# Sums over five chunks in one PSUM bank at loaded addresses, 16 single table lines a chunk and 72 VectorE column copies

## The chip, the core and the metric

The kernel runs on one core of a Trainium2 chip. The metric is the device time of one execution in microseconds (us). Five engines work beside each other, each through its own queue in order: TensorE (PE, with its weight loads shown as PEld), VectorE (DVE), ScalarE (ACT), GpSimd (POOL) and SyncE (SP). In this kernel POOL and SP only issue transfers once the main loop runs.

## What is computed

A graph layer with 12,500 nodes of 48 features and 400,000 edges, sorted by their target node `dst`. The source nodes `src` are random.

```python
h = jnp.maximum(_layernorm(x), 0.0)
tmp = jnp.concatenate([h[dst], h[src], edge_attr], axis=1)   # 48 + 48 + 32
hid = jax.nn.relu(tmp @ W1 + b1)                             # 128 wide
msg = hid @ W2 + b2
x = x + jax.ops.segment_sum(msg, dst, num_segments=12500)
```

Since W1 acts on three parts apart, the kernel first makes two node tables: `tab_a` (W1's part for `dst`, with b1) and `tab_b` (its part for `src`). The product with W2 is taken after the sum over the edges of a node: the sum of `hid` and the number of edges (for b2) are all that it needs.

## The kernel before

**Stages.** `node_tables` makes the two tables in DRAM, and a transposed copy `bt` of `tab_b` in SBUF. Then `windows` runs over 391 chunks of 1,024 edges, a chunk being 8 tiles (`T`) of 128 edges. As the edges are sorted, the targets of a chunk lie within a window of 80 nodes (`W`).

**One chunk.** SP brings 80 rows of `tab_a` (`rhs`), the edge features (`lhs`, rows 80 to 111) and the targets (`row`). DVE compares the targets with the window's nodes into the other rows of `lhs` (line 458) and into `hot`, a 0/1 matrix of edges by window nodes (line 464; its other operand `wnum`, the numbers of the window's nodes, lies in a PSUM bank of its own). PE multiplies `lhs` and `rhs` into `pre` (`before`, line 476). DVE adds the rows of `tab_b` and applies the maximum with 0 into `hid` (lines 506, 513 and 515). PE multiplies `hid` with `hot` (`fold`, line 524) for the sums of `hid` by node, and `ones` with `hot` (line 529) for the numbers of edges.

**Three ways to bring a row of `tab_b`.** Most tiles of a chunk are gathered by POOL, one indirect transfer a tile (line 442; 2,631 in all). 458 tiles are brought as columns of `bt` that are copied one by one within SBUF (line 384): 151 columns a chunk, 71 by DVE and 80 by ACT, in nine parts (`PARTS`). Each part first reads its columns' addresses into registers (line 349, TENSOR_LOAD). PE turns such a tile and adds it to `pre` (`turned`, line 485). 36 tiles are brought by SP, line by line: 12 transfers of 512 bytes a chunk (`singles`, line 416), which DVE adds to `pre` (line 504).

**The sum over chunks.** `fold` leaves the sums of one chunk in a fresh PSUM tile `p_g`. DVE adds it into `seg`, a buffer in SBUF of 1,024 nodes, at the window's place (`add`, line 543). After 12 chunks (`GQ`) DVE moves the overlap to the other buffer and clears the rest (`segment_next`, lines 559 and 561). PE multiplies the buffer with W2, half by half (`segment_sum`, lines 569 and 570), DVE adds that to `xseg`, the segment's part of x (line 571), and SP stores it (line 575) after having loaded it (line 552).

**Order.** The order is written out by hand: in the pass for chunk c the engines make `prepare(c)` (transfers, `lhs`, `hot`), `before(c-1)`, `fold(c-2)`, `turned(c-1)`, the segment's work, `gathered(c-1)`, `hidden(c-1)` and `add(c-2)`, with the column copies between them. SP's transfers share eight completion semaphores in turn, so each waits until the one eight before it has landed. `rhs` has three buffers, as has `lhs`; `gb`, where POOL's rows land, has eight; a column tile `gt` five.

Of the kernel before, what the change touches and what calls it, by code (L numbers as in the profile page):

```python
# [16 lines left out]
P = 128  # L17
# [12 lines left out]
GQ = 12  # L30
OFF = -(NCH - 3) % GQ
L = 1024
# [3 lines left out]
BLK = 512  # L36
STORE = 2
# [18 lines left out]
    (True, 0, 19, 1),  # L56
    (True, 19, 20, 20),
    (True, 39, 16, 40),
    (True, 55, 16, 56),
    (False, 71, 16, 72),  # L60
    (False, 87, 16, 88),
    (False, 103, 16, 104),
    (False, 119, 16, 120),
    (False, 135, 16, 136),
# [6 lines left out]
SEG0 = 130848  # L71
SEG_SIZE = 8 * L
# [3 lines left out]
PLACE0 = 156  # L76
SINGLE = 12
SINGLE_AT = 160
WIDTH = 172
# [199 lines left out]
def windows(nc, tc, gp, bt, ident, idx, x_t, tab_a, tab_b, dst, edge_t, w1, w2s, b2s, out_t):  # L279
# [3 lines left out]
    with ExitStack() as es:  # L283
        seg = es.enter_context(tc.tile_pool(name="segs", bufs=1))

        segs = [seg.tile([P, 2, L], F32, name=f"seg{k}") for k in range(2)]
# [6 lines left out]
        ps_g = es.enter_context(tc.tile_pool(name="ps_g", bufs=2, space=PSUM))  # L293
        ps_f = es.enter_context(tc.tile_pool(name="ps_f", bufs=1, space=PSUM))
        xp = es.enter_context(tc.tile_pool(name="xp", bufs=2))
        ps_w = es.enter_context(tc.tile_pool(name="ps_w", bufs=1, space=PSUM))


        wnum = ps_w.tile([P, W], F32, name="wnum")
# [16 lines left out]
        place = PARTS[0][3] - 1  # L316
        for a, b in ((place, SEG2), (NEXT, SEG)):
# [4 lines left out]
        at_place = slice(place, place + 1)  # L322
        nc.vector.scalar_tensor_tensor(
            last[:, :, at_place], last[:, :, at_place], 4.0, last[:, :, PLACE0 : PLACE0 + 1],
            op0=ALU.mult, op1=ALU.add,
        )
        for seg in segs:
            nc.vector.memset(seg, 0.0)
# [9 lines left out]
        def group(c):  # L338

            return divmod(c + OFF, GQ)  # L340

        def begin(g):
            return max(0, g * GQ - OFF)

        def numbers(c, at, n, engine):

            got = []
            for k in range(0, n, MOST):
                got += nc.values_load_multi_w_load_instructions(  # L349
                    last[c % P : c % P + 1, c // P, at + k : at + min(k + MOST, n)],  # L350
                    engines=[engine], min_val=0, max_val=1 << 23,
                    skip_runtime_bounds_check_because="numbers of nodes, and what is made of them",
                )[1]
            return got

        def node(n):
            return n.with_bounds(min_val=0, max_val=N - 1)
# [3 lines left out]
        def load(c, part):  # L361

            dve, first, n, at = PARTS[part]
            n = max(0, min(n, len(BYCOLS) * P - ((c - COLS) * PART + first))) if c >= COLS else 0
            engine = mybir.EngineType.DVE if dve else mybir.EngineType.Activation
            if part == 0 and 2 <= c < NCH + 2:
                base, *nodes = numbers(c, at - 1, n + 1, engine)
                st[c - 2]["base"] = base
            else:
                nodes = numbers(c, at, n, engine) if n else []  # L370
            regs[c, part] = nodes
# [19 lines left out]
        def mark(ins, us):  # L391
            marks.append((ins, us))
# [77 lines left out]
        def before(c):  # L470

            s = st[c]
            n = s["n"]
            pre = ps_p.tile([P, T, HID], F32, name="pre")
            for t in range(n):
                nc.tensor.matmul(  # L476
                    pre[:, t, :], s["lhs"][:K, t * P : (t + 1) * P], s["rhs"][:K, :],
                    start=True, stop=t not in turned_at(c),
                )
            s["pre"] = pre  # L480
# [37 lines left out]

        def fold(c):
            s = st[c]  # L520
            n = s["n"]
            p_g = ps_g.tile([HID, 2, W], F32, name="p_g")
            for t in range(n):
                nc.tensor.matmul(  # L524
                    p_g[:, 0, :], s["h"][:, t, :], s["hot"][:, t, :], start=t == 0, stop=t == n - 1
                )
            high = s["hot"].bitcast(BF16)
            for t in range(n):
                nc.tensor.matmul(  # L529
                    p_g[:, 1, :], ones, high[:, t, 1::2], start=t == 0, stop=t == n - 1  # L530
                )
            s["p_g"] = p_g

        def add(c):

            s = st.pop(c)
            k = group(c)[0] % 2
            of = SEG0 + k * SEG_SIZE
            at = s["base"].with_bounds(
                min_val=of, max_val=of + 4 * FAR, guaranteed_mod_val=0, out_of_modulus=4  # L540
            ) - of
            to = segs[k].bitcast(U8)[:, :, bass.ds(at, 4 * W)].bitcast(F32)
            mark(nc.vector.tensor_add(to, to, s["p_g"]), 0.25)  # L543

        xs = {}
# [8 lines left out]
        def segment_next(g):  # L554

            old, new = segs[g % 2], segs[(g + 1) % 2]
            if g > 0:
                for k in range(2):
                    nc.vector.memset(new[:, k, W:], 0.0)  # L559
            of, = numbers(begin(g), NEXT, 1, mybir.EngineType.DVE)  # L560
            nc.vector.tensor_copy(
                new[:, :, :W], old[:, :, bass.ds(of.with_bounds(min_val=0, max_val=FAR), W)]
            )

        def segment_sum(g, k, n):

            seg, s = segs[g % 2], slice(k * BLK, k * BLK + n)
            p_f = ps_f.tile([D, BLK], F32, name="p_f")
            nc.tensor.matmul(p_f[:, :n], w2s, seg[:, 0, s], start=True, stop=False)  # L569
            nc.tensor.matmul(p_f[:, :n], b2s[:1, :], seg[:1, 1, s], start=False, stop=True)  # L570
            nc.vector.tensor_add(xs[g][:, s], xs[g][:, s], p_f[:, :n])  # L571

        def segment_store(g, n):
            first, = numbers(begin(g), SEG, 1, mybir.EngineType.SP)
            nc.sync.dma_start(out_t[:, bass.ds(node(first), n)], xs.pop(g)[:, :n])

        with tc.manual_schedule():
            for c in range(NCH + 2):
# [8 lines left out]
                if 0 <= c - 1 < NCH:  # L587
                    before(c - 1)
                if 0 <= c - 2 < NCH:
                    fold(c - 2)  # L590
                if 0 <= c - 1 < NCH:
                    turned(c - 1)

                g, k = group(c - 2)
                if k == GQ - 3 or c == NCH - 1:
                    segment_load(g)
                if g > 0 and k < L // BLK:
                    segment_sum(g - 1, k, BLK)
# [9 lines left out]
                if 0 <= c - 2 < NCH:  # L608
                    add(c - 2)
                    if k == GQ - 1:  # L610
                        segment_next(g)
                columns(c, 3)
                for part in range(DVE_PARTS, len(PARTS)):
                    load(c, part)
                    columns(c, part)
                if c == NCH + 1:
                    segment_sum(g, 0, END_L)
                    segment_store(g, END_L)
# [342 lines left out]
```

## Time and profile before

| | us |
|---|---|
| median of 3 runs | 3562.99 (3554.6 to 3570.09) |
| the profiled execution | 3548.53 |
| its span, first to last instruction | 3546.7 |
| busy: PE / DVE / ACT / POOL | 2628.1 / 3258.7 / 3123.8 / 2667.2 |
| DVE column copies (27,584) / ACT column copies (31,040) | 1818.8 / 3077.3 |
| mean granted TensorE clock | 0.784 of full |

Durations of successive instructions of an engine overlap a little, so what one costs is read from its start to the next one's start. SP has no line of busy time; the timeline shows the transfers that it issues, each with the time that the issue took. A bracket at the end of a timeline row gives the idle time ahead of it and what ended it.

### The profile page before, as it was taken

How to read it: one execution, taken by the hardware profiler on the slowest of the kernel's cores; microseconds unless marked ns; L12 is line 12 of the kernel's file. 1: busy time of each engine (PE TensorE's matmuls, PEld its weight loads, DVE VectorE, ACT ScalarE, POOL GpSimd, SP SyncE). 2: the span in 40 equal slices, each digit the busy share in tenths (PEclk: the TensorE clock that was granted, in tenths of full speed). 3: DMA queues.
4: the chain of work that ended last, by engine and by line, in shares of the span. 5: the costliest groups of instructions: out<-in, count | busy, mean ns of one | idle time of the engine just before them, and what ended most of it. 6: DMA issues, size and time to landing. Idle time of an engine off the chain costs nothing.

```text
span 3546.7 us, 119948 instructions
## 1 busy us (share of the span) xinstructions
PE 2628.1 (74%) x17111; PEld 2359.2 (67%) x17111; DVE 3258.7 (92%) x30218; ACT 3123.8 (88%) x31115; POOL 2667.2 (75%) x2658
## 2 busy tenths in 40 slices
PE   8677677777777776777777777777777777777777
PEld 6566666667666766666667666666666666666666
DVE  6799999999999999999999999999999999999997
ACT  5898989899898898988999899998988899898884
POOL 5777777777777777777777777777777777777773
PEclk9677887786777778877787778777787788777777
DMA  5533333333333333333333333333333333333332
GB/s 201 164 97 99 96 93 94 93 93 102 95 93 92 95 90 103 95 96 93 92 95 97 97 96 96 95 92 93 99 95 93 95 91 93 103 96 94 91 95 58
DMA packets 197246, 349.05 MB, mean 98 GB/s; under 512 B 67763, under 2 KB 104517, under 8 KB 195157
## 3 DMA queue, kind: packets, MB, share of 16 engines
q0 software_dynamic: 84224, 172.62, 19.2%
q1 hardware_dynamic: 111952, 168.56, 15.8%
q14 instruction: 670, 5.48, 0.5%
q8 instruction: 140, 2.29, 0.3%
q10 hardware_dynamic: 260, 0.10, 0.0%
HBM read 321.55 MB, written 22.07 MB: 97 GB/s over the span
## 4 chain that ended last, share of the span: by engine, by line
DVE 68%; PE 8%; ACT 6%; issue 5%; DVEq 4%; DMA 3%; SPq 0%; ACTq 0%; POOL 0%; POOLq 0%
DVE gt L384 38%; DVE hid L506 8%; ACT gt L384 6%; DVE hot L464 6%; DVE lhs L458 5%; DVE hid L513 5%; DVEq L349 4%; PE p_g L524 4%; DMA gb<-tab_b,srci 3%; DVE seg L543 2%; DVE hid L515 2%; PE p_f L569 1%; PE p_f L570 1%; PE pre L476 1%; PE pre L485 1%
## 5 line engine op out<-in xcount | busy, mean ns | idle before, releaser
L384 ACT COPY gt<-bt 128x1 f32 x31040 | 3077.3, 187 | 334.0 <-PE pre L485 226.2
L442 POOL DMA_INDIRECT gb<-tab_b,srci x2631 | 2645.7, 1006 | 822.5 <-issue 371.7
L384 DVE COPY gt<-bt 128x1 f32 x27584 | 1818.8, 144 | 161.1 <-issue 104.3
L524 PE MATMUL p_g<-hot,hid 128*128 128x80 f32 x6250 | 1074.6, 344 | 873.8 <-DVE hid L513 873.4
L524 PEld LDWEIGHTS p_g<-hot,hid 128*128 128x128 f32 x6250 | 1004.6, 252 | 950.1 <-DVE hid L513 940.9
L476 PEld LDWEIGHTS pre<-rhs,lhs 112*128 112x128 f32 x6250 | 964.9, 243 | 86.1 <-issue 85.2
L476 PE MATMUL pre<-rhs,lhs 112*128 112x128 f32 x6250 | 994.1, 327 | 16.5 <-DMA lhs<-in_edge_t 16.3
L506 DVE TENSOR_TENSOR hid<-pre,gb 128x896 f32<-128x896 f32 (+2 forms) x391 | 408.7, 1045 | 0.6
L464 DVE TENSOR_TENSOR hot<-wnum,rel 128x640 f32<-128x640 f32 x391 | 318.2, 814 | 0.0
L458 DVE TENSOR_SCALAR lhs<-row,bw 80x1024 f32<-80x1024 int16 x391 | 290.2, 742 | 9.2 <-DMA row<-in_dst 9.2
L485 PE MATMUL pre<-ident,gt 128*128 128x128 f32 x916 | 270.2, 403 | 9.8 <-DVE gt L384 9.6
L513 DVE TENSOR_SCALAR hid<-hid 128x896 f32<-128x896 f32 (+2 forms) x391 | 243.0, 622 | 0.1
L529 PE MATMUL p_g<-hot,ones 128*128 128x80 bf16 x3125 | 239.4, 237 | 0.0
L529 PEld LDWEIGHTS <-ones 128*128 128x128 bf16 x3125 | 239.1, 132 | 0.0
L485 PEld LDWEIGHTS pre<-ident,gt 128*128 128x128 f32 x916 | 192.4, 269 | 11.2 <-issue 11.2
L543 DVE TENSOR_TENSOR seg<-seg,p_g 128x160 f32 x391 | 124.5, 318 | 15.1 <-issue 11.4
L515 DVE TENSOR_SCALAR hid<-pre 128x128 f32<-128x128 f32 (+1 forms) x389 | 118.7, 305 | 0.0
L569 PE MATMUL p_f<-seg,w2s 128*48 128x512 f32 (+1 forms) x134 | 106.5, 890 | 0.4 <-DVE seg L543 0.4
L571 DVE TENSOR_TENSOR xseg<-xseg,p_f 48x512 f32<-48x512 f32 (+1 forms) x67 | 45.0, 672 | 50.8 <-PE p_f L570 50.7
L570 PE MATMUL p_f<-seg,b2s 1*48 1x512 f32 (+1 forms) x134 | 86.6, 731 | 0.0
L570 PEld LDWEIGHTS p_f<-seg,b2s 1*48 1x48 f32 x134 | 12.4, 135 | 87.6 <-issue 87.6
L559 DVE MEMSET seg<- 128x944 f32 x64 | 54.1, 845 | 9.3
(67 smaller groups left out, 294.7 us busy)
## 6 DMA issues: line engine op xcount, KB each, us to landing
gr<-tab_b SPq DMA_DIRECT2D x4608, 0.5 KB
row<-in_dst SPq DMA_DIRECT2D x390, 160.0 KB
lhs<-in_edge_t SPq DMA_DIRECT2D x390, 128.0 KB
gb<-tab_b,srci POOLq DMA_INDIRECT x2631
rhs<-tab_a SPq DMA_DIRECT2D x391, 40.0 KB
xseg<-in_x_t SPq DMA_DIRECT2D x33, 192.0 KB
out_x<-xseg SPq DMA_DIRECT2D x33, 192.0 KB
tab_b<-tab SPq DMA_DIRECT2D x3, 1280.0 KB
```

What stands on the lines that cost most here:

```text
L384: done = copy(gts[of][:, e : e + 1], bt8[:, bass.ds(at, 4)].bitcast(F32))
L442: fetch = nc.gpsimd.indirect_dma_start(out=gb[:, t, :], out_offset=None, in_=tab_b[:, :], in_offset=bass.IndirectOffsetOnAxis(ap=srci[:, c ...
L458: mark(nc.vector.tensor_scalar(lhs[:W, : n * P], row[:, : n * P], bw[:, c : c + 1], None, op0=ALU.is_equal,), 0.8)
L464: mark(nc.vector.tensor_tensor(hot[:, :n, :], wnum.unsqueeze(1).to_broadcast([P, n, W]), rel[:, c * T : c * T + n].unsqueeze(2).to_broadca ...
L476: nc.tensor.matmul(pre[:, t, :], s["lhs"][:K, t * P : (t + 1) * P], s["rhs"][:K, :], start=True, stop=t not in turned_at(c),)
L485: nc.tensor.matmul(st[c]["pre"][:, t, :], gts.pop(j), ident, start=False, stop=True)
L506: mark(nc.vector.tensor_add(to, of, rows), 1.0)
L513: mark(nc.vector.tensor_scalar(of, of, 0.0, None, op0=ALU.max), 0.55)
L515: nc.vector.tensor_scalar(apart(c, s["h"], True), apart(c, s["pre"], True), 0.0, None, op0=ALU.max)
L524: nc.tensor.matmul(p_g[:, 0, :], s["h"][:, t, :], s["hot"][:, t, :], start=t == 0, stop=t == n - 1)
L529: nc.tensor.matmul(p_g[:, 1, :], ones, high[:, t, 1::2], start=t == 0, stop=t == n - 1)
L543: mark(nc.vector.tensor_add(to, to, s["p_g"]), 0.25)
```

## The change

- **Fewer chunks to a segment, and the sum on PE.** A segment is now 5 chunks and 432 nodes. Its sums lie in one PSUM bank (`sums`), the edge numbers in another (`degs`), two of each in turn. `segment_begin` clears both by a product of zeros. `fold` reads two addresses into PE's registers and adds each product into the bank there. `add` and `segment_next` are gone.
- **The segment's end.** ACT copies the banks to SBUF (`segment_copy`, first chunk of the next segment), PE multiplies with W2 into the same bank (`segment_product`, second chunk), DVE copies the 80 overlapping nodes from the last `xseg` and adds the product (`segment_sum`, third chunk), SP stores it in the fifth. Before, store and load came once in 12 chunks; now each comes once in 5.
- **Where a row comes from.** `SINGLE` goes from 12 to 16 lines a chunk, DVE's columns from 71 to 72. 48 tiles come by lines, 461 by columns and 2,616 by POOL. DVE's parts are 16, 20, 20 and 16 columns, where they were 19, 20, 16 and 16.
- **One bank shared.** `wnum`, which `hot` is made from, now lies in the bank of the first of the two `degs` (tile `deg0`).

```diff
-GQ = 12
+GQ = 5
-L = 1024
+L = 432
-STORE = 2
+STORE = 4
...
-SINGLE = 12
+SINGLE = 16
...
+        sums = [ps_s.tile([P, L], F32, name=f"sum{k}") for k in range(2)]
+        beside = ps_w.tile([P, L + W], F32, name="deg0")
+        degs = [beside[:, :L], ps_w.tile([P, L], F32, name="deg1")]
+        wnum = beside[:, L:]
...
+        def segment_begin(g):
+            for of in (sums[g % 2], degs[g % 2]):
+                nc.tensor.matmul(
+                    of, zeros[:, :P], zeros, start=True, stop=False, skip_group_check=True
+                )
...
         def fold(c):
...
-            p_g = ps_g.tile([HID, 2, W], F32, name="p_g")
+            for at, of, first in zip(
+                numbers(c, PLACE, 2, mybir.EngineType.PE), (sums[k], degs[k]),
...
+                to.append(of.bitcast(U8)[:, bass.ds(at, 4 * W)].bitcast(F32))
             for t in range(n):
                 nc.tensor.matmul(
-                    p_g[:, 0, :], s["h"][:, t, :], s["hot"][:, t, :], start=t == 0, stop=t == n - 1
+                    to[0], s["h"][:, t, :], s["hot"][:, t, :], start=False, stop=False,
...
-            mark(nc.vector.tensor_add(to, to, s["p_g"]), 0.25)
...
+        def segment_copy(g):
+            sm[g] = segp.tile([P, 2, L], F32, name="seg")
+            nc.scalar.copy(sm[g][:, 0, :], sums[g % 2])
+            nc.scalar.copy(sm[g][:1, 1, :], degs[g % 2][:1, :])
...
+        def segment_product(g, n):
+            seg, p_f = sm.pop(g), out_of(g, n)
+            nc.tensor.matmul(p_f, w2s, seg[:, 0, :n], start=True, stop=False, skip_group_check=True)
...
+        def segment_sum(g, n):
             if g > 0:
-                for k in range(2):
-                    nc.vector.memset(new[:, k, W:], 0.0)
...
+                nc.vector.tensor_copy(
+                    xs[g][:, :W],
+                    xs[g - 1][:, bass.ds(of.with_bounds(min_val=0, max_val=FAR), W)],
+                )
+            nc.vector.tensor_add(xs[g][:, :n], xs[g][:, :n], out_of(g, n))
```

**On SP**, a chunk's transfers and a store of a segment in the middle of the loop, before (line 416 brings single lines, line 575 stores):

```order
L427 DMA rhs_717<-tab_a 80x512
L432 DMA lhs<-in_edge_t 32x1024
L434 DMA row<-in_dst 80x1024
L349 TENSOR_LOAD last
L416 DMA gr<-tab_b 1x512 x12
L349 TENSOR_LOAD last
L575 REGISTER_ALU
L575 DMA out_x<-xseg 48x1024
```

and with the change (lines 411 and 582):

```order
L422 DMA rhs_712<-tab_a 80x512
L427 DMA lhs<-in_edge_t 32x1024
L429 DMA row<-in_dst 80x1024
L349 TENSOR_LOAD last
L411 DMA gr<-tab_b 1x512 x16
L349 TENSOR_LOAD last
L582 REGISTER_ALU
L582 DMA out_x<-xseg 48x432
```

The row of lines grew from 12 to 16; a store (and a load, written alike) stands there every fifth chunk, with a read of a number ahead of it.

**On PE**, one chunk's `before` and the start of its `fold`, with the semaphores waited for, before:

```order
L476 MATMUL pre_25892<-rhs0_713,lhs_25166 128x128 x7
L524 MATMUL p_g_25901<-hot_24681,hid_25366 128x80 [waits DVE_49]
L524 MATMUL p_g_25901<-hot_24681,hid_25366 128x80 x6
L524 MATMUL p_g_25901<-hot_24681,hid_25366 128x80 [waits DVE_49]
L529 LDWEIGHTS ones_88
L529 MATMUL p_g_25901<-hot_24681,ones_88 128x80
```

and with the change, in a segment that uses `deg0`:

```order
L471 MATMUL pre_24982<-rhs0_712,lhs_24229 128x128 x7
L349 TENSOR_LOAD last_87
L535 MATMUL sum0_690<-hot_23718,hid_24444 128x80 [waits DVE_49]
L535 MATMUL sum0_690<-hot_23718,hid_24444 128x80 x6
L535 MATMUL sum0_690<-hot_23718,hid_24444 128x80 [waits DVE_49]
L541 LDWEIGHTS ones_88
L541 MATMUL deg0_692<-hot_23718,ones_88 128x80 [waits DVE_49]
```

A read of two addresses stands between `before` and `fold`, and the first product into `deg0` waits for DVE, where line 529 waited for nothing more. Segments that use `deg1` have no such wait.

**On DVE**, from `hidden` to the next `hot`, before:

```order
L513 TENSOR_SCALAR hid_52569<-hid_52569 128x896
L515 TENSOR_SCALAR hid_52569<-pre_52542 128x128
L349 TENSOR_LOAD last_87
L543 TENSOR_TENSOR seg0_663<-seg0_663,p_g_52551 128x2x80
L384 COPY gt_52539<-bt_58 128x1 x16
L458 TENSOR_SCALAR lhs_52921<-row_52923,bw_85 80x1024
```

and with the change, from `hidden` to the segment's sum in the third chunk of a segment:

```order
L510 TENSOR_SCALAR hid_58276<-pre_58243 128x128
L349 TENSOR_LOAD last_87
L379 COPY gt_58238<-bt_58 128x1 x16
L453 TENSOR_SCALAR lhs_58639<-row_58641,bw_85 80x1024
L459 TENSOR_TENSOR hot_58701<-deg0_692,rel_84 128x640
L379 COPY gt_58692<-bt_58 128x1 x20
L349 TENSOR_LOAD last_87
L574 ISA
L574 COPY xseg_55985<-xseg_53118 48x80
L578 TENSOR_TENSOR xseg_55985<-xseg_55985,sum1_691 48x432
```

The addition into `seg` is gone from every chunk; `hot` reads the tile that PE's line 541 writes, and the overlap's copy and one addition stand in one chunk of five.

More of the change, by code (lines that the diff above doesn't have):

```diff
@@ L314, in windows @@
         taba8 = tab_a.rearrange("n h -> (n h)").bitcast(U8)
[L316 to L317 removed]
+        for a, b in ((PLACE, SEG2), (PLACE + 1, SEG2), (NEXT, SEG)):
             nc.vector.tensor_tensor(
@@ L365, in load @@
             engine = mybir.EngineType.DVE if dve else mybir.EngineType.Activation
[L366 to L371, printed above, removed]
+            regs[c, part] = numbers(c, at, n, engine) if n else []
         def columns(c, part):
@@ L529, in fold @@
                 nc.tensor.matmul(
-                    p_g[:, 1, :], ones, high[:, t, 1::2], start=t == 0, stop=t == n - 1
+                    to[1], ones, high[:, t, 1::2], start=False, stop=False, skip_group_check=True
                 )
[L532 to L545, printed above, removed]
+        xs, sm = {}, {}
         def segment_load(g):
@@ L912 @@
     nxt = first[np.minimum(of * GQ - OFF + GQ, NCH - 1)]
-    numbers[2 : NCH + 2, PARTS[0][3] - 1] = first
-    numbers[2 : NCH + 2, SEG2] = seg
-    numbers[2 : NCH + 2, PLACE0] = SEG0 + of % 2 * SEG_SIZE
+    for k, of0 in enumerate((SUM0, DEG0)):
+        numbers[:NCH, PLACE + k] = first
+        numbers[:NCH, PLACE0 + k] = of0 + of % 2 * SUM_SIZE
+    numbers[:NCH, SEG2] = seg
     numbers[:NCH, BASE] = first
```

100 lines of the change are left out of this document (52 added, 48 removed).

## The prediction

> **What bounds the kernel now.** I read the chain of the page first, then DVE's timeline, then SP's and POOL's, since they only issue and have little in the table of busy times.
>
> ```profile
> DVE 68%; PE 8%; ACT 6%; issue 5%; DVEq 4%; DMA 3%; SPq 0%; ACTq 0%; POOL 0%; POOLq 0%
> ```
>
> The chain runs over DVE for two thirds of the span, and neither SP nor POOL is on it. One chunk in DVE's timeline (start, duration, what it is), and the comparison into `lhs` for chunks 8 and 385:
>
> ```profile
> 1805.85 0.32 DVE L543 TENSOR_TENSOR seg<-seg,p_g 128x160 f32 x1
> 1806.09 1.05 DVE L384 COPY gt<-bt 128x1 f32 x16
> 1807.07 0.74 DVE L458 TENSOR_SCALAR lhs<-row,bw 80x1024 f32<-80x1024 int16 x1
> 1807.95 1.25 DVE L384 COPY gt<-bt 128x1 f32 x19
> 1809.11 0.81 DVE L464 TENSOR_TENSOR hot<-wnum,rel 128x640 f32<-128x640 f32 x1
> 1811.34 1.09 DVE L506 TENSOR_TENSOR hid<-pre,gb 128x896 f32<-128x896 f32 x1
> ...
> 172.97 0.74 DVE L458 TENSOR_SCALAR lhs<-row,bw 80x1024 f32<-80x1024 int16 x1
> ...
> 3482.97 0.73 DVE L458 TENSOR_SCALAR lhs<-row,bw 80x1024 f32<-80x1024 int16 x1
> ```
>
> DVE goes from one instruction to the next without a gap that another engine ends. From chunk 8 to 385 it takes 3310.0 us for 377 chunks, 8.78 a chunk. So DVE sets the pace, and what is taken off it counts, until another engine is as slow. That is the question here, so the others come next.
>
> **SP** has waits in front of its store, and after each it catches up at its own speed:
>
> ```profile
> SPq L575 <- DVE xseg L571: 403.3, 30, 25.7
> ...
> 1012.23 0.33 SPq L427 DMA_DIRECT2D rhs<-tab_a  x1
> ...
> 1046.79 0.32 SPq L427 DMA_DIRECT2D rhs<-tab_a  x1
> ...
> 1821.83 0.32 SPq L427 DMA_DIRECT2D rhs<-tab_a  x1
> ...
> 1822.67 0.41 SPq L434 DMA_DIRECT2D row<-in_dst  x1
> 1824.00 3.86 SPq L416 DMA_DIRECT2D gr<-tab_b  x12
> 1828.61 0.32 SPq L427 DMA_DIRECT2D rhs<-tab_a  x1
> ...
> 1857.46 0.33 SPq L427 DMA_DIRECT2D rhs<-tab_a  x1
> ...
> 1859.63 4.30 SPq L416 DMA_DIRECT2D gr<-tab_b  x12
> ...
> 1892.62 0.32 SPq L427 DMA_DIRECT2D rhs<-tab_a  x1
> ```
>
> The two stretches from `rhs` to `rhs`, at 1012.23 and 1857.46, are five chunks each behind a store: 34.56 and 35.16 us, together 6.97 a chunk. That is SP when it waits for no engine, 1.81 us below DVE's pace. 12 lines take 3.86 to 4.30 us, so 0.322 to 0.358 each; I take 0.335.
>
> **POOL and ACT**, in their groups, with the last gather and the addition that uses it:
>
> ```profile
> L442 POOL DMA_INDIRECT gb<-tab_b,srci x2631 | 2645.7, 1006 | 822.5 <-issue 371.7 <-DVE gt L384 180.8 <-DMA gb<-tab_b,srci 124.4
> L384 ACT COPY gt<-bt 128x1 f32 x31040 | 3077.3, 187 | 334.0 <-PE pre L485 226.2 <-issue 62.0 <-DMA gb<-tab_b,srci 5.0
> ...
> 3497.52 0.95 POOL L442 DMA_INDIRECT gb<-tab_b,srci  x1 [0.30 <-DVE gt L384]
> ...
> 3534.38 0.81 DVE L506 TENSOR_TENSOR hid<-pre,gb 128x640 f32<-128x640 f32 x1
> ```
>
> A gather takes POOL (2645.7 + 822.5) / 2631 = 1.32 us with the gap behind it, from first to last. It ends 36 us ahead of the addition that needs it: not a bound, but not far. ACT waits 226.2 us for PE to release `gt`, 0.58 us a chunk, so it needs some 8.2.
>
> **The change, part by part. DVE** loses the addition (1805.85 to 1806.09: 0.24 us in 391 chunks, 94 us) and the clearing of the buffers; the end of a segment changes:
>
> ```profile
> L559 DVE MEMSET seg<- 128x944 f32 x64 | 54.1, 845 | 9.3
> L571 DVE TENSOR_TENSOR xseg<-xseg,p_f 48x512 f32<-48x512 f32 (+1 forms) x67 | 45.0, 672 | 50.8 <-PE p_f L570 50.7
> ```
>
> The clearing is 54 us. The additions stay at some 44 (78 of 672 ns x 432/512, for 45.0); their wait for PE, 51, goes, as a chunk now lies between product and addition. One column more is 16 in 0.98 us (1806.09 to 1807.07), 0.061 a chunk, 24. The overlap's copy with its number has no row: from 0.18 us (a few of these columns) to 1.2 (20 columns that don't hide the read) each, 78 times; I take 0.4, near the gap of 0.14 that the reads ahead of 1807.95 leave, 31 us (14 to 94). In sum 94 + 54 + 1 + 51 - 24 - 31 = 145 us less, 0.37 a chunk: DVE would need 8.41.
>
> **SP** gets more. Per chunk: 4 lines x 0.335 = 1.34. Reading 16 numbers for 12: the gap ahead of the lines is 0.92 us (1823.08 to 1824.00), that ahead of `rhs` with one number 0.75, so 11 numbers cost 0.17 and 4 cost 0.06. 6.97 + 1.40 = 8.37. Each segment has a load and a store, priced by a load that waited for nothing:
>
> ```profile
> 2108.48 0.32 SPq L427 DMA_DIRECT2D rhs<-tab_a  x1
> ...
> 2115.30 0.32 SPq L552 DMA_DIRECT2D xseg<-in_x_t  x1
> 2116.11 0.32 SPq L427 DMA_DIRECT2D rhs<-tab_a  x1
> ```
>
> 7.63 us for this chunk; without the load the best are some 6.78 (1821.83, the row of lines at 1824.00 behind it, to 1828.61), so 0.85. A store reads a number and waits in two places; I take 0.9 (0.7 to 1.2). (0.85 + 0.9) / 5 = 0.35. **SP needs 8.72 a chunk**, above DVE's 8.41 and under 8.78. The store's wait is gone: the sum is made in a segment's third chunk and stored in the fifth. SP is then what ends last, and DVE waits for `row` at its comparison.
>
> The loop's start is slower, for the copies of x go out beside it:
>
> ```profile
> 102.50 0.34 SPq L427 DMA_DIRECT2D rhs<-tab_a  x1
> ...
> 104.91 4.49 SPq L416 DMA_DIRECT2D gr<-tab_b  x12
> ...
> 160.00 0.33 SPq L427 DMA_DIRECT2D rhs<-tab_a  x1
> ...
> 107.14 0.75 DVE L458 TENSOR_SCALAR lhs<-row,bw 80x1024 f32<-80x1024 int16 x1 [1.22 <-DMA row<-in_dst]
> ```
>
> Seven chunks in 57.5 us, 8.21 each; four lines more at 4.49/12 = 0.374 and the reading make 9.77. `rhs` of chunk 8 is issued at 102.50 + 68.4 = 170.9, and of chunk 385 at 170.9 + 377 x 8.72 = 3458.3. DVE's comparison that waited for `row` began 4.64 us after that chunk's `rhs` (102.50 to 107.14): 3463, where it was 3482.97. **20 us less.** The last six chunks have no lines, so DVE sets their pace as before; there a clearing and some waits for PE go, and ACT's copies come in, which I put at 4 us less. Span 3546.7 - 24 = 3522.7.
>
> **PE, ACT, POOL.** PE in a chunk at the lower clock, the groups of the W2 products, the mean clock, and an ACT copy from PSUM:
>
> ```profile
> 1814.21 3.07 PE L524 MATMUL p_g<-hot,hid 128*128 128x80 f32 x16 [4.05 <-DVE hid L513]
> 1817.07 0.74 PE L529 MATMUL p_g<-hot,ones 128*128 128x80 bf16 x8
> 1817.61 0.78 PE L485 MATMUL pre<-ident,gt 128*128 128x128 f32 x2
> 1818.18 3.62 PE L476 MATMUL pre<-rhs,lhs 112*128 112x128 f32 x16
> ...
> L569 PE MATMUL p_f<-seg,w2s 128*48 128x512 f32 (+1 forms) x134 | 106.5, 890 | 0.4 <-DVE seg L543 0.4
> L570 PE MATMUL p_f<-seg,b2s 1*48 1x512 f32 (+1 forms) x134 | 86.6, 731 | 0.0
> ...
> core 0: 3546.7 us, clock 0.784
> ...
> L234 ACT COPY tab<-p_n 128x512 f32<-128x512 f32 x33 | 19.0, 586 | 20.4 <-PE p_n L225 18.1 <-DMA tab_a<-tab 1.3 <-DVE bw L878 0.7
> ```
>
> PE's work is 7.6 us (1814.21 to 1821.80) of 8.1. The read of two addresses has no row on PE; on SP one number takes about 0.75 us. It stands behind `before`, where PE then waits for `hid` (4.05 us ahead of this `fold`), so I take nothing; with that cover gone it is up to 0.75 a chunk, and less than nothing is excluded, as it only adds. Products at loaded addresses have no row either: I take the old duration; nothing makes them quicker, and the second rival prices them a quarter slower. Line 541's new wait is for `hot` of the current pass, since `hot` reads that tile. Queued behind it are 0.74 us of products and `turned`, 0.78, which line 506 on DVE waits for. Between the end of `hot` (1809.92) and line 506 DVE has 1.42 us of copies: so 0.1 late at the low clock, up to 0.9 in a chunk that turns two tiles, in half of the segments. That is some 0.1 a chunk, which the 0.3 that DVE has under SP hides. The W2 product keeps its size (78 times 432 columns for 67 times 512), and the zeros lie in PE's waits. ACT makes two copies a segment, at most 586 ns x 432/512 = 0.49 each: 0.2 a chunk, so 8.4, and under SP. POOL makes 15 gathers less, 20 us.
>
> A rule speaks against the lines. The Trainium skill, "DMA: Bandwidth & Descriptors", Rules for kernel authors, says to coalesce small transfers, since below 64 KB one pays mostly overhead. By the fixed cost of some 2 us that its Anatomy of one DMA gives, four lines more would be an estimated 8 us a chunk if they followed each other, some 3,000 us in all; by the row at 1824.00, twelve in 3.86 us, they overlap, and SP's issue is all that a line costs here.
>
> **The rivals.**
> - **SP is cheaper than that, and POOL ends last** (15%). SP's price rests on the lines' mean; at 0.322, with store and load at 0.7 each, it is 8.60 a chunk, 45 us less in 377. DVE alone would give 3546.7 - 145 = 3402. But POOL is then the floor: last gather 20 us earlier, and the 36 us of lead used up but for some 3: 3546.7 - 20 - 33 = 3494. It decides once SP needs under 8.64. Time 3510 by the scale below. For it: SP's best chunks, 6.78; against it: ten in a row made 6.97.
> - **PE's products at loaded addresses are slower, and the kernel with them** (22%). A quarter more on 3.07 + 0.74 makes 8.55 of the low clock's 7.6. The W2 products, (106.5 + 86.6) us for 67 halves, are 2.9 a half, 2.4 a segment at 432 columns, and with the zeros an estimated 0.6 a chunk: 9.15, against SP's 8.72. If the low clock is about half of full, the mean of 0.784 makes it two chunks in five: 0.43 x 391 x 0.4 = 67 us over the forecast, 3606. It decides from a seventh more (8.2 + 3.81 x 0.14 = 8.72), where PE at the low clock passes SP. For it: `turned`, and line 506 with it, now stand behind `hot`. Against it: the 4.05 us that PE waits here.
> - **SP as priced** (63%).
>
> **How the numbers follow.** The profiled execution took 3548.53, 1.8 more than its span, and the median is 3562.99, 1.0041 of it. (3522.7 + 1.8) x 1.0041 = **3539**. The four lines at 0.322 to 0.358 are worth 20 us down and 35 up in 377 chunks, load and store some 25 either way. So SP's own case reaches from 3510, where POOL takes over, to 3600, and holds both signs: of its 63 in 100, 30 lie under 3545 (faster by over 0.5%, about what a measurement of this kernel can tell from no change), 26 within 0.5%, and 7 above 3581. POOL's 15 are 12 faster and 3 within, PE's 22 are 4 within and 18 slower. Together 0.42, 0.33 and 0.25. The range is 3500 to 3612: a little under POOL's floor, whose lead I took from one row, and a little over PE's price.
>
> **What would show it.** SP without waits at its store, 16 lines in 5.2 to 5.5 us, 8.7 us from `rhs` to `rhs`; DVE idle before its comparison with `row` as what ends it, some 0.2 to 0.3 a chunk; line 543 gone. If instead DVE waits for PE at line 501, the second rival holds; if for `gb`, the first. The forecast is wrong if a line's issue is not 0.33 us when SP never rests, or if DVE's 0.37 isn't there.

## The result, and the profile after

The changed kernel takes **3702.88 us** (median of 4 runs, 3699.03 to 3708.69) where the kernel before takes 3558.8 beside it: a ratio of **1.0406**, with an interval of 1.0368 to 1.0444. The forecast was 3539 us, in a range of 3500 to 3612. So the kernel is slower, by 144 us, where it was to be 20 us faster.

From the page of the changed kernel: the chain by engine, and groups of instructions (busy time, mean ns, then the idle time ahead of them and what ended most of it):

```profile
DVE 59%; PE 17%; issue 8%; DVEq 6%; DMA 5%; POOL 2%; ACT 2%; SPq 1%; ACTq 0%; POOLq 0%
...
L437 POOL DMA_INDIRECT gb<-tab_b,srci x2616 | 2571.2, 983 | 970.5 <-issue 469.1
L379 ACT COPY gt<-bt 128x1 f32 x31040 | 3069.3, 187 | 111.0 <-issue 67.3
L379 DVE COPY gt<-bt 128x1 f32 x27968 | 1845.9, 144 | 256.8 <-issue 235.9
L535 PE MATMUL sum<-hot,hid 128*128 128x80 f32 x6250 | 1063.7, 341 | 436.1 <-DVE hid L508 431.4
L501 DVE TENSOR_TENSOR hid<-pre,gb 128x896 f32<-128x896 f32 (+2 forms) x391 | 407.6, 1043 | 170.7 <-PE pre L480 159.4
L541 PE MATMUL deg<-hot,ones 128*128 128x80 bf16 x3125 | 245.1, 242 | 185.4 <-DVE hot L459 181.8
L558 ACT COPY seg<-deg 1x432 f32<-1x432 f32 x79 | 39.9, 506 | 319.8 <-DVE hot L459 297.0
L517 PE MATMUL deg<-zeros 1*128 1x432 bf16 x79 | 37.4, 473 | 228.7 <-DVE hot L459 228.7
```

PE's share of the chain has doubled (8 to 17%), and DVE now waits 159.4 us for `turned` (line 480) ahead of its addition at line 501, and 25.7 us ahead of the one at line 499. Three groups wait for `hot`: `fold` at line 541, which the prediction named, and two that it didn't: **the zeros product into `deg0` (228.7 us)** and ACT's copy at line 558. The place in the timelines of PE and of DVE, at the first chunk of a segment that sums in `deg0` (every tenth chunk):

```profile
1749.02 3.20 PE L471 MATMUL pre<-rhs,lhs 112*128 112x128 f32 x16
1752.15 0.35 PE L517 MATMUL sum<-zeros 1*128 1x432 bf16 x1
1756.62 0.51 PE L517 MATMUL deg<-zeros 1*128 1x432 bf16 x1 [4.12 <-DVE hot L459]
1757.22 3.67 PE L535 MATMUL sum<-hot,hid 128*128 128x80 f32 x16
1760.69 0.74 PE L541 MATMUL deg<-hot,ones 128*128 128x80 bf16 x8
1761.23 0.78 PE L480 MATMUL pre<-ident,gt 128*128 128x128 f32 x2
```

```profile
1754.02 0.74 DVE L453 TENSOR_SCALAR lhs<-row,bw 80x1024 f32<-80x1024 int16 x1
1754.78 1.06 DVE L379 COPY gt<-bt 128x1 f32 x16
1755.76 0.81 DVE L459 TENSOR_TENSOR hot<-deg,rel 128x640 f32<-128x640 f32 x1
1756.76 1.30 DVE L379 COPY gt<-bt 128x1 f32 x20 [0.19 <-issue]
1762.04 1.09 DVE L501 TENSOR_TENSOR hid<-pre,gb 128x896 f32<-128x896 f32 x1 [3.97 <-PE pre L480]
1763.53 1.30 DVE L379 COPY gt<-bt 128x1 f32 x20 [0.40 <-issue]
...
1766.45 0.74 DVE L453 TENSOR_SCALAR lhs<-row,bw 80x1024 f32<-80x1024 int16 x1
...
1774.95 0.76 DVE L453 TENSOR_SCALAR lhs<-row,bw 80x1024 f32<-80x1024 int16 x1
```

`hot` reads `wnum`, which lies in the tile `deg0`. The zeros product writes that tile, and stands ahead of `fold` and `turned` in PE's queue. PE has nothing left to do at 1752.5 and waits until `hot` is done at 1756.57. Then come 4.8 us of products until line 480 is done (1757.22 to 1762.01), and DVE, which has 1.3 us of copies to cover them, stands still for 3.97 us. That chunk takes 12.43 us (1754.02 to 1766.45), the next one 8.50.

SP isn't what ends last, although its work is as priced. Its rows (start, duration, transfer), and its wait for the sum at its store:

```profile
1804.62 0.41 SPq L429 DMA_DIRECT2D row<-in_dst  x1
1806.21 5.15 SPq L411 DMA_DIRECT2D gr<-tab_b  x16
...
1812.97 0.32 SPq L422 DMA_DIRECT2D rhs<-tab_a  x1
...
1821.37 0.32 SPq L422 DMA_DIRECT2D rhs<-tab_a  x1
```

```profile
SPq L582 <- DVE xseg L578: 7.3, 2, 6.0
```

A chunk without load or store takes SP 8.40 us (1812.97 to 1821.37). The wait of the store for the sum, 403.3 us before, is down to 7.3; one more store waited 25.7 us, for the overlap's copy at line 574.

### The profile page after: what moved, and what is told of

The parts are those of the page before. It is cut to its first block, busy times and chain, and to the rows that moved or that the text cites. A ratio compares the mean times of both kernels' runs of the same rounds, so it can differ in the third digit from the quotient of the medians.

```text
span 3697.3 us, 124404 instructions
## 1 busy us (share of the span) xinstructions
PE 2808.7 (76%) x17323; PEld 2481.9 (67%) x17323; DVE 3167.2 (86%) x30215; ACT 3181.9 (86%) x31273; POOL 2593.1 (70%) x2644
## 4 chain that ended last, share of the span: by engine, by line
DVE 59%; PE 17%; issue 8%; DVEq 6%; DMA 5%; POOL 2%; ACT 2%; SPq 1%; ACTq 0%; POOLq 0%
DVE gt L379 34%; DVE hid L501 7%; PE sum L535 7%; DVE hot L459 6%; DVEq L349 5%; DVE lhs L453 5%; DVE hid L508 5%; DMA gb<-tab_b,srci 4%; PE pre L471 3%; POOL gb L437 2%; ACT gt L379 2%; PE pre L480 2%; DVE hid L510 2%; PE deg L541 2%; PE p_n L226 1%
## 5 line engine op out<-in xcount | busy, mean ns | idle before, releaser
L437 POOL DMA_INDIRECT gb<-tab_b,srci x2616 | 2571.2, 983 | 970.5 <-issue 469.1
L379 DVE COPY gt<-bt 128x1 f32 x27968 | 1845.9, 144 | 256.8 <-issue 235.9
L535 PEld LDWEIGHTS sum<-hot,hid 128*128 128x128 f32 x6250 | 1002.2, 251 | 769.4 <-DVE hid L508 496.8
L535 PE MATMUL sum<-hot,hid 128*128 128x80 f32 x6250 | 1063.7, 341 | 436.1 <-DVE hid L508 431.4
L471 PEld LDWEIGHTS pre<-rhs,lhs 112*128 112x128 f32 x6250 | 1068.8, 266 | 96.7 <-issue 96.7
L471 PE MATMUL pre<-rhs,lhs 112*128 112x128 f32 x6250 | 1097.4, 350 | 17.4 <-DMA lhs<-in_edge_t 17.4
L501 DVE TENSOR_TENSOR hid<-pre,gb 128x896 f32<-128x896 f32 (+2 forms) x391 | 407.6, 1043 | 170.7 <-PE pre L480 159.4
L541 PE MATMUL deg<-hot,ones 128*128 128x80 bf16 x3125 | 245.1, 242 | 185.4 <-DVE hot L459 181.8
L459 DVE TENSOR_TENSOR hot<-deg,rel 128x640 f32<-128x640 f32 x391 | 318.0, 813 | 0.0
L558 ACT COPY seg<-deg 1x432 f32<-1x432 f32 x79 | 39.9, 506 | 319.8 <-DVE hot L459 297.0
L517 PE MATMUL deg<-zeros 1*128 1x432 bf16 x79 | 37.4, 473 | 228.7 <-DVE hot L459 228.7
L566 PE MATMUL sum<-seg,w2s 128*48 128x432 f32 (+1 forms) x158 | 100.8, 730 | 0.5 <-ACT seg L557 0.5
L567 PE MATMUL sum<-seg,b2s 1*48 1x432 f32 (+1 forms) x158 | 100.9, 728 | 0.0
L557 ACT COPY seg<-sum 128x432 f32<-128x432 f32 x79 | 40.2, 509 | 34.0 <-issue 17.0
```

Of the source, the lines that this page charges most:

```text
L379: done = copy(gts[of][:, e : e + 1], bt8[:, bass.ds(at, 4)].bitcast(F32))
L437: fetch = nc.gpsimd.indirect_dma_start(out=gb[:, t, :], out_offset=None, in_=tab_b[:, :], in_offset=bass.IndirectOffsetOnAxis(ap=srci[:, c ...
L459: mark(nc.vector.tensor_tensor(hot[:, :n, :], wnum.unsqueeze(1).to_broadcast([P, n, W]), rel[:, c * T : c * T + n].unsqueeze(2).to_broadca ...
L471: nc.tensor.matmul(pre[:, t, :], s["lhs"][:K, t * P : (t + 1) * P], s["rhs"][:K, :], start=True, stop=t not in turned_at(c),)
L501: mark(nc.vector.tensor_add(to, of, rows), 1.0)
L535: nc.tensor.matmul(to[0], s["h"][:, t, :], s["hot"][:, t, :], start=False, stop=False, skip_group_check=True,)
```

## The experiments

Kernels were run on the chip of the comparison above, here A, and on five others, B to F, each time beside the kernel before on the same chip. Which chip A is isn't known, so it may be one of the five. The chips differ: the kernel before takes 3554.7 to 3558.8 us on A, D and F, and 4414.7 to 4476.0 on B, C and E. So ratios are compared, and those of A, D and F apart from those of B, C and E.

| kernel | chip, before there (us) | time (us) | ratio to before |
|---|---|---|---|
| changed | A, 3558.8 | 3702.9 | 1.0406 (1.0368 to 1.0444) |
| `wnum` in SBUF | D, 3554.7 | 3587.2 | 1.0093 (1.0073 to 1.0114) |
| and other parts | D | 3586.7 | 1.0095 (1.0073 to 1.0116) |
| and 72 columns on ACT | D | 3596.0 | 1.0115 (1.0096 to 1.0133) |
| `wnum` in SBUF, 12 lines | F, 3555.7 | 3575.3 | 1.0057 (1.0040 to 1.0074) |
| and other parts | F | 3588.4 | 1.0082 (1.0049 to 1.0114) |
| zeros early | B, 4419.5 | 4417.3 | 0.9997 (0.9987 to 1.0007) |
| `wnum` in SBUF | B | 4416.8 | 0.9996 (0.9985 to 1.0008) |
| 12 lines | B | 4487.4 | 1.0150 (1.0133 to 1.0166) |
| other parts | B | 4507.1 | 1.0201 (1.0184 to 1.0218) |
| changed | C, 4476.0 | 4552.8 | 1.0171 (1.0149 to 1.0194) |
| `wnum` in SBUF | C | 4478.6 | 1.0004 (0.9991 to 1.0017) |
| and other parts | C | 4513.4 | 1.0086 (1.0067 to 1.0106) |
| and other parts, 12 lines | C | 4497.5 | 1.0056 (1.0028 to 1.0084) |
| `wnum` in SBUF, 12 lines | E, 4414.7 | 4402.6 | 0.9971 (0.9956 to 0.9985) |
| and other parts | E | 4418.4 | 1.0009 (0.9995 to 1.0024) |
| 12 lines, bank shared | E | 4479.1 | 1.0144 (1.0119 to 1.0168) |
| before, with 16 lines | E | 4427.6 | 1.0029 (1.0014 to 1.0044) |

### The first four: bank, lines, parts

The theories after the comparison were the shared bank (PE's wait for `hot`), SP's lines, and DVE's reads of addresses. The edits, in the first four runs each made alone to the changed kernel:

```diff
 # zeros early: the zeros go to the start of the pass, ahead of prepare(c) and its hot
+                if 0 <= c - 2 < NCH and c - 2 == begin(g):
+                    segment_begin(g)
                 if c < NCH:
                     prepare(c)
...
-                    if c - 2 == begin(g):
-                        segment_begin(g)
                     fold(c - 2)
 # wnum in SBUF
-        wnum = beside[:, L:]
+        wnum = one.tile([P, W], F32, name="wnum")
 # 12 lines
-SINGLE = 16
+SINGLE = 12
 # other parts: 20, 20, 16 and 16 columns
-    (True, 0, 16, 0),
-    (True, 16, 20, 16),
-    (True, 36, 20, 36),
+    (True, 0, 20, 0),
+    (True, 20, 20, 20),
+    (True, 40, 16, 40),
 # later, 72 columns on ACT: 24 tiles move to POOL's gathers
-    (False, 136, 16, 136),
+    (False, 136, 8, 136),
```

> The two products of zeros that open a segment are issued at the start of their pass, ahead of the pass's comparison into hot, so that the one into deg0 waits for the hot of the pass before. Theory A (bank): the changed kernel loses its time where that product waits for hot of the same pass, since wnum lies in deg0's bank: 40 waits of PE, 228.7 us in all, behind which fold and turned stand; DVE's chunk at that place takes 12.67 us where the others take 8.45. Then this kernel is faster than the changed one by 4.2 us in 39 places, some 165 us: about 3540. Theory B (lines): SP's 16 lines a chunk set the pace: within 0.5% of the changed kernel's 3703. Theory C (number reads): DVE lost its gain to the read of 20 addresses behind line 501: also 3703.

> wnum, the window's node numbers, is put into SBUF, so that it shares no PSUM bank; nothing else is changed. Theory A (bank): all waits of PE and ACT for hot go (228.7 us for the zeros, 181.8 us for the products of line 541, 297 us for ACT's copy); the 165 us of the segment's first chunk come back as in the kernel with early zeros, and a little more where line 541 was late: 3520 to 3545, unless hot itself becomes slower when it reads SBUF (813 ns now; 0.1 us more would cost 39 us). Theories B (lines) and C (number reads): 3703 within 0.5%.

> The changed kernel with 12 lines a chunk on SP, as before the change; POOL gathers the tiles that are no longer brought by lines (12 more gathers). Theory B (lines): SP's 16 lines set the pace, so 4 x 0.33 = 1.3 us a chunk less on SP lets DVE go at its own: 3703 falls by 100 us or more. Theories A (bank) and C (number reads): SP is not what ends last (rhs is issued some 10 us ahead of its use), so 3703 within 0.5%.

> The changed kernel with DVE's 72 columns in parts of 20, 20, 16 and 16, so that 16 addresses, not 20, are read behind line 501 (16 to 20 in the changed kernel's order of 16, 20, 20, 16). Theory C (number reads): from the start of line 501 to the next instruction DVE takes 1.40 us where it took 1.00; 0.3 to 0.4 us a chunk come back, 100 to 150 us: about 3570 to 3600. Theory A (bank): the gap behind line 501 closes, but where the first chunk of a segment waits nothing changes; with DVE's ordinary chunk shorter by 0.3 us, still some 60 to 120 us faster: so this run tells C's size, not A from C. Theory B (lines): 3703 within 0.5%.

The times expected were those of chip A, and this was chip B, without the changed kernel beside them. In ratios the two that take the wait of the zeros away stand at 1.000, the two that leave it at 1.015 and 1.020. That fits the bank, but lacks its control, which came next. With the zeros early, line 541 still waits 225.1 us, and the kernel is as fast as the one with `wnum` in SBUF, where line 541 doesn't wait: of the waits for `hot`, the zeros' is the one that costs there.

### The control, and the edits on top of each other

> The changed kernel itself, as a control, since the chips differ: on the chip of the first comparison the kernel before took 3558.8 us and this one 1.0406 of it; on the chip of the first four experiments the kernel before took 4419.5 us, and two variants of this one stood at 1.000 and two at 1.015 and 1.020. Expected by the theory of the shared bank (PE's zeros wait for hot of the current pass, 4.2 us in every tenth chunk): 1.04 of before where the chip is as fast as the first, and 1.015 to 1.02 where it is as slow as the second, that is, like the two variants there that kept the bank shared. If instead it stands at 1.00 on the slow chip, the two variants at 1.015 and 1.020 were slowed by their own edits, and the shared bank costs nothing there. In the profile the zeros into deg0 should show some 200 to 300 us of waiting for hot.

> The changed kernel with wnum in SBUF instead of beside deg0. Shared bank: the wait of the zeros for hot and ACT's wait for hot ahead of its second copy both go, DVE's addition at line 501 waits for turned under 60 us in all instead of 170, and the time falls by some 39 x 4.2 = 165 us where a chunk takes 8.4 us (ratio to before 0.99 to 1.00), and by 1.5 to 2% on the slow chip (ratio 1.000). SP as the bound (the prediction's theory): nothing changes, the ratio stays that of the changed kernel run beside it. Reads of numbers on DVE: nothing changes either.

> wnum in SBUF, and DVE's parts as 20, 20, 16 and 16 columns, so that 16 addresses instead of 20 are read behind line 501 and 20 instead of 16 behind line 453. Reads of numbers: on the fast chip line 501 to the next instruction goes from 1.40 to 1.00 us and line 453 from 0.75 to 0.92, 0.24 a chunk or some 90 us less than the same kernel with only wnum moved (2.5% less; with SP the bound at 8.7 a chunk this gain would be cut to nothing). Shared bank alone: no difference from the kernel with only wnum moved. On the slow chip, where the two engines stand still together for other reasons, under 1%.

> The last one with 12 lines a chunk instead of 16, so 12 tiles more are gathered by POOL and 12 fewer brought by SP. If SP's queue sets the pace once the bank and the reads are out of the way (8.7 us a chunk with 16 lines, 7.3 with 12), this is faster by up to 0.3 us a chunk, some 3%. If SP isn't the bound, the time is the same within 0.5%, or slower by some 10 us because POOL makes 12 gathers more.

The changed kernel stands at 1.0171 on chip C, `wnum` in SBUF at 1.0004: the shared bank costs 74 us there, all that the change costs. If the changed kernel stands on B as it does on C, the 12 lines and the other parts gained nothing on B. The other parts made the kernel with `wnum` in SBUF 0.8% slower on C, which none of the theories expected, and 12 lines on top of them brought 1.0086 to 1.0056, with intervals that overlap.

### The same on a chip like the first

> The changed kernel with wnum in SBUF again, in case this chip is as fast as the first (before some 3560 us; the other two took 4420 and 4476). On such a chip the changed kernel stood at 1.0406. Shared bank: 37 zeros products of 4.2 us each and what ACT loses there go, 155 to 165 us, so 0.995 to 1.00 of before. If the shared bank is worth there only what it is worth on the slower chip (4553 to 4479, 74 us), the ratio is 1.02. If SP's queue or the reads of numbers make up the loss, 1.03 to 1.04. On a slow chip: 1.000 again.

> The kernel before, for its profile on this chip. On a slow chip, theory: ACT's 80 columns a chunk set the pace, since ACT and DVE both stand still between copies with no releaser (issue, some 950 and 820 us in the changed kernel); then ACT waits for next to nothing but issue here too, and that would be why this kernel and the one with wnum in SBUF take the same time. Rival: DVE sets it, then DVE's waits for other engines are near nothing and ACT waits some 200 us for PE as on the first chip. On a fast chip: the profile shown before, span near 3547.

> wnum in SBUF, and 72 columns a chunk on ACT instead of 80 (144 in all, so 24 tiles move from the columns to POOL's gathers). If ACT sets the pace on a slow chip, 2 to 4% faster than the kernel with only wnum moved, until DVE is as late; if it doesn't, the same within 0.5%. On a fast chip ACT has some 0.3 us a chunk to spare, so this gives nothing there, and POOL's 24 gathers at 1.32 us may cost up to 32 us (0.9%).

> wnum in SBUF and parts 20, 20, 16, 16. On a fast chip, theory of the reads of numbers: 16 addresses instead of 20 behind line 501 spare 0.40 us there and cost 0.16 behind line 453, 0.24 a chunk, some 90 us or 2.5% under the kernel with only wnum moved; if SP is by then the bound at 8.7 us a chunk, nothing. On a slow chip 0.8% slower, as before.

Chip D is like A. `wnum` in SBUF brings the ratio from 1.0406 to 1.0093: **the shared bank costs 0.031, some 111 us** of the 144. The changed kernel itself ran on A and C alone, so this size rests on two chips that take the same time for the kernel before; on C both ran on one chip. `hot` takes 813 ns with `wnum` in either place, so the move itself costs DVE nothing. The ratio was expected to be 1.00, though, so something else holds this kernel. ACT doesn't: it waits 191.1 us for `fold` ahead of its copies at line 557. The run with fewer columns on ACT gives nothing either, but can't show that alone, since its 24 more gathers keep POOL at work until 3580.25, 17 us from the end of the span. Waits of DVE, ACT and SP in the kernel with `wnum` in SBUF (us in total, times, longest), DVE's comparisons of chunks 8 and 385, and SP's rows:

```profile
DVE gt L379 <- issue: 261.8, 929, 0.8
DVE lhs L453 <- DMA row<-in_dst: 43.1, 47, 13.9
...
DVE hid L501 <- PE pre L480: 14.3, 17, 2.7
...
ACT seg L557 <- PE sum L535: 191.1, 67, 12.7
...
SPq L422 <- PE pre L471: 12.1, 10, 6.0
```

```profile
176.59 0.75 DVE L453 TENSOR_SCALAR lhs<-row,bw 80x1024 f32<-80x1024 int16 x1 [2.39 <-DMA row<-in_dst]
...
3525.11 0.79 DVE L453 TENSOR_SCALAR lhs<-row,bw 80x1024 f32<-80x1024 int16 x1
```

```profile
1814.27 0.36 SPq L427 DMA_DIRECT2D lhs<-in_edge_t  x1
1814.68 0.41 SPq L429 DMA_DIRECT2D row<-in_dst  x1
1816.23 5.15 SPq L411 DMA_DIRECT2D gr<-tab_b  x16
1822.14 0.32 SPq L422 DMA_DIRECT2D rhs<-tab_a  x1
```

The wait for line 480 is down from 159.4 to 14.3 us, and now DVE waits for `row`, as the prediction had it, though for 0.11 us a chunk (43.1 / 391) where 0.2 to 0.3 were forecast. A chunk takes 8.88 us ((3525.11 - 176.59) / 377). Reading 16 numbers leaves 1.14 us ahead of the lines (1815.09 to 1816.23), where 12 left 0.92. The other parts changed nothing, which fits SP (it leaves DVE to wait) but doesn't show it.

### SP's lines alone

> wnum in SBUF and 12 lines a chunk instead of 16 (12 tiles more by POOL, 2,628 gathers). On a chip with before near 3555. If SP's queue is what holds the kernel with wnum in SBUF at 1.0093 of before (a chunk of 8.87 us, the lead of row on DVE's comparison down to some 3 us), SP needs 8.87 - 4 x 0.33 - 0.23 for the reads = 7.3 us, DVE 8.45 in an ordinary chunk and 8.6 in the mean, and POOL, 2,628 gathers of 1.32 us, becomes as late as in the kernel before: 3500 to 3540, ratio 0.985 to 0.995. If DVE's reads hold it instead, the ratio stays at 1.005 to 1.01. On a slow chip (before 4420 or 4476): 1.000, and the same as with 16 lines.

> The last one with DVE's parts 20, 20, 16 and 16. With 16 lines these parts gave nothing (1.0095 against 1.0093), which would be SP's doing: DVE's comparison waited for row instead. If so, with 12 lines the order of parts may give up to 0.1 to 0.2 us a chunk over the one with parts 16, 20, 20 and 16, as far as POOL allows (ratio 0.98 to 0.99). If the order of the reads is worth nothing in itself (what one line gains another loses), the two are equal within 0.3%.

> The changed kernel as it is, bank shared, with 12 lines instead of 16. If the shared bank holds SP's cost hidden, this stays near the changed kernel's 1.0406 (1.03 to 1.045) although the same edit brings 1.5 to 2% or more where wnum is in SBUF. If the two costs add up, it is 1.015 to 1.02.

> The kernel before with 16 lines a chunk instead of 12, and nothing else (12 tiles fewer by POOL). SP needs 6.97 + 4 x 0.33 + 0.23 = 8.5 us a chunk, and its load and store come once in 12 chunks; DVE needs 8.78. But SP also waits there for a store, up to 25 us once in 12 chunks, and must then catch up at 0.3 us a chunk instead of 1.8. If SP's queue costs nothing as long as its sum is under DVE's, the ratio is 0.997 to 1.003. If the waits at the store are then no longer caught up, 30 stores of some 10 to 13 us that show make 1.02 to 1.10.

> wnum in SBUF with 12 lines again, in case this chip is as fast as the first. If SP's queue holds the kernel with wnum in SBUF and 16 lines at 1.0093 of before, this takes 3500 to 3540 us, ratio 0.985 to 0.995, with DVE's waits for row gone and row's lead back at 5 us or more. If not SP, 1.005 to 1.01. On a slow chip: 0.997, as before.

> The same with DVE's parts 20, 20, 16 and 16. If the order of the reads is worth something once SP is out of the way, faster than the one with parts 16, 20, 20 and 16 by up to 2%, as far as POOL allows; if what one line gains another loses, equal within 0.3%. On a slow chip 0.4% slower, as before.

The first four of these went to chip E. Against the ratios of B and C, 12 lines gain 0.3% with `wnum` in SBUF (1.000 to 0.9971) and nothing to speak of with the bank shared. 16 lines cost the kernel before 0.3%, and the other parts make the kernel with 12 lines 0.4% slower. On F, like A, 12 lines bring 1.0093 (on D) to 1.0057, some 13 us, where 1.4 to 2.4% were expected; the intervals of the two just meet, so the waits have to say what changed. Waits of the kernel with `wnum` in SBUF and 12 lines:

```profile
DVE gt L379 <- issue: 235.3, 828, 1.2
DVE hid L501 <- DMA gb<-tab_b,srci: 47.2, 44, 6.3
...
DVE lhs L453 <- DMA row<-in_dst: 14.6, 3, 12.9
...
SPq L422 <- PE pre L471: 491.8, 186, 9.1
```

SP now waits for others: 491.8 us until `rhs` is free, where the kernel with 16 lines waited 12.1. DVE's wait for `row` is down from 43.1 to 14.6 us, and DVE waits 47.2 us for `gb`, POOL's gathers. **So SP had next to no time to spare with 16 lines and has with 12, and close behind SP stands the next bound, POOL.** DVE's comparisons of chunks 8 and 385 make 8.85 us a chunk:

```profile
169.17 0.74 DVE L453 TENSOR_SCALAR lhs<-row,bw 80x1024 f32<-80x1024 int16 x1
...
3505.28 0.76 DVE L453 TENSOR_SCALAR lhs<-row,bw 80x1024 f32<-80x1024 int16 x1
```

Without its waits for `gb` (47.2 / 391) DVE needs some 8.73, while POOL needs 2,628 / 391 gathers of 1.32 us, 8.87. POOL's idle time in this kernel, and its last gather:

```profile
POOL gb L437 <- issue: 445.7, 1461, 0.5
...
3556.97 0.94 POOL L437 DMA_INDIRECT gb<-tab_b,srci  x1 [0.30 <-issue]
```

From the second gather to the last, no gap between two gathers is over 0.33 us, so POOL never rests. Its last gather starts 16 us before the end of the span (3573.2), where the one of the kernel before starts 49 us before it (3497.52 of 3546.7): POOL's lead is used up. Why POOL is late shows at the start, in POOL's timeline before:

```profile
29.03 1.19 POOL L844 DMA_INDIRECT spare<-in_x,srci  x1 [0.19 <-issue]
50.74 0.96 POOL L442 DMA_INDIRECT gb<-tab_b,srci  x1 [20.52 <-DMA tab_b<-tab]
```

and with the change:

```profile
30.34 1.19 POOL L855 DMA_INDIRECT spare<-in_x,srci  x1 [0.18 <-issue]
90.84 0.45 POOL L301 MEMSET zeros<- 1x432 bf16 x1 [59.31 <-ACT tab L235]
91.77 0.95 POOL L437 DMA_INDIRECT gb<-tab_b,srci  x1 [0.49 <-issue]
```

The one clearing of `zeros` waits 59.31 us for a table copy of ACT, and the first gather goes out at 91.77 instead of 50.74. POOL, which never rests in the kernel before either, starts **41 us later**. In the changed kernel the bank's waits hide this: POOL itself waits there, 145.6 us for line 501 alone. What an earlier start would be worth was not tried (with the clearing on DVE, say), so it stays argued; POOL without a rest and DVE's 47.2 us of waiting for `gb` are what the run shows.

## Why the prediction was wrong

- **The step that failed: "the zeros lie in PE's waits".** The text found the new dependency on `hot`, but only for line 541, with two short products behind it, and priced it at 0.1 us a chunk under SP. The zeros into `deg0` write the same tile, stand ahead of all of `fold` and of `turned`, and so hold line 501 up by 4 us in every tenth chunk. PE's wait did not lie beside other work: line 501 stands behind it. 37 to 40 such chunks of some 4 us are 150 to 160 us; with the dependency gone, 0.031 of the ratio is gone, 111 us, and SP is then the next that is late. The Trainium skill, "PSUM — Partial Sum Buffer", section "PSUM bank collisions raise a hardware error", asks for semaphores by bank and quadrant, not by address, with two reads counted too. The trace agrees with what that makes of a shared bank: ACT's copy at line 558 waits 297.0 us for `hot`, though both only read. With that rule each of the three groups could have been listed beforehand.
- **DVE's 0.37 a chunk (145 us): the parts removed are right, the sum is not.** The addition and the clearing of buffers are gone, but DVE's idle time ahead of its column copies has grown. The kernel before, on A and on D:

```profile
L384 DVE COPY gt<-bt 128x1 f32 x27584 | 1818.8, 144 | 161.1 <-issue 104.3
...
DVE gt L384 <- issue: 101.5, 403, 3.5
```

On A this idle time goes from 161.1 us in all to 256.8, of which the waits with no releaser go from 104.3 to 235.9 (short gaps are in the first figure alone). 96 us more are 0.24 a chunk, two thirds of the gain. With `wnum` in SBUF it is 284.5 us on D and 252.8 on F. The idle time stands where a part's addresses are read: at 1763.53 above 0.40 us of it behind line 501, where 20 addresses are read instead of 16. The other parts, which read 16 there and 20 behind line 453, show that it goes with the number of addresses: added up over the trace, it falls from 118 to 30 us behind line 501 on D, and grows from 61 to 183 behind line 453. So what one line gains the other loses, and the kernel is as fast as before (1.0095 to 1.0093). On F the sum falls from 252.8 to 230.3 us, but there DVE waits 67.7 us for POOL instead of 47.2, and the ratios are 1.0082 and 1.0057, with intervals that overlap. How to get this time back is open.
- **SP's 8.72 a chunk was right, but not as the kernel's pace.** It didn't set the pace of the changed kernel. The kernel with `wnum` in SBUF goes at 8.88, and of that SP waits for other engines for 0.14 (53 us in 377 chunks, added up over the trace), so its own work is 8.74. Mis-sized in it was the reading of 16 numbers, 0.06 more a chunk by interpolation from one to twelve: it is 0.22 (1.14 for 0.92). A line, at 0.322 (16 in 5.15) instead of 0.335, makes up for part of that. The sum took SP's work for the pace and put its waits at nothing. At 8.88 instead of 8.72, 377 chunks take 60 us more, nearly all by which the span of that kernel (3584.3) is longer than the forecast's 3522.7.
- **The products at loaded addresses** are not a quarter slower. Their group has, in the kernel before,

```profile
L524 PE MATMUL p_g<-hot,hid 128*128 128x80 f32 x6250 | 1074.6, 344 | 873.8 <-DVE hid L513 873.4
```

a mean of 344 ns, at a mean granted clock of 0.784. With the change it has 341 at 0.733, and with `wnum` in SBUF on D 357 at 0.760: nowhere near the quarter more that the second rival priced. So the rival that forecast a slower kernel had the right sign and place (line 501 waiting for `turned`) by luck: the cause is another.
- **POOL's floor of 3510** in the first rival took POOL's start as before. With the start 41 us later it lies near 3550, and 12 gathers more of 1.32 us make 3567 for the kernel with 12 lines, which took 3575.
- **Off the path after all:** the W2 products and ACT's copies. DVE waits 4.7 us in all for the products at its addition in line 578 in the changed kernel, and ACT waits 191.1 us for `fold` ahead of its copies in the kernel with `wnum` in SBUF on D.

That the zeros' wait is the cost is shown by taking it away in two ways (another place for `wnum`, another place for the zeros, equal on B); its 4 us are read from A's timelines. No version here beats the kernel before on a chip like A; the best is at 1.0057. On the slower E that one stands at 0.9971.

## What to carry to other kernels

When two things come to share a buffer or a bank, list every instruction that writes it, not only the one in the diff that looks costly, and look at what is queued behind each of them: a wait of 4 us in one chunk of ten was worth 3% of the kernel. Where engines lie within 0.2 us a chunk of one another (here SP 8.88 with 16 lines, POOL 8.87 and DVE 8.73 with 12), taking one bound away shows the next, and little of the gain is left. And a clearing that runs once can make an engine that never rests afterwards start 41 us late, if it stands ahead of that engine's first work.

## What the runs showed beside that

**The chips differ by a quarter in the same kernel.** The kernel before takes 3555 us on D and 4476 on C. A column copy takes as long on both (187 ns in ACT's groups), but on C ACT and DVE stand still between copies with no releaser. ACT's and DVE's waits in the kernel with `wnum` in SBUF on C, then ACT's on D:

```profile
ACT gt L379 <- issue: 980.1, 2290, 4.3
...
DVE gt L379 <- issue: 826.1, 1842, 1.4
```

```profile
ACT gt L379 <- issue: 75.7, 252, 4.3
```

What ends these waits is not in the records, and its cause is open. On such a chip ACT waits for hardly anything else, so that ACT with its 80 columns may set the pace there and hide part of what a change on other engines does; the run that was to test it (72 columns on ACT) went to D, and leaves it open. The same edit is worth 3.1% on A and D, and 1.7% on C.
